# Selective-scan, attention and FFN block: delta split by half-words on VectorE, backward scans that start from the forward y, and a remade plan

## The chip, the core and the metric

The kernel runs on one core of a Trainium2 chip. The metric is the device time of one execution in microseconds (us); a version's time is the median of several runs. A profiled execution is one run more, whose trace is read here.

## What is computed

The input is `x` of 8 images, 96 channels, 64 x 64 points, f32. Layer 0 is a group norm, then a state-space block in four directions, added to `x`; layer 1 is linear attention over the 4096 points of an image and a quantized FFN, each added. What the change touches is in the state-space block:

```python
xs = stack([x_hw, x_wh]); xs = concatenate([xs, flip(xs)])     # 4 directions k: rows, columns, and both reversed
x_dbl = einsum('bkdl,kcd->bkcl', xs, x_proj_w)
dts, Bs, Cs = split(x_dbl, [6, 22], axis=2)
delta = softplus(einsum('bkrl,kdr->bkdl', dts, dt_proj_w) + dt_proj_b)
# scan over l: h = exp(delta * A) * h + delta * u * B;  y = sum_n h * C
out_y = scan(...) + D * u
y = out_y[:, 0] + inv_y[:, 0] + wh_y + invwh_y                 # directions 0 + 2 (reversed) + 1 + 3 (reversed)
y = layernorm(y) * silu(z);  out = y @ out_proj_w.T
```

There are 192 channels d, 16 states n and 4096 points l per direction. The four y's of a point are summed before the layer norm.

## The kernel before

The images are worked in four pairs. For each pair there is a **planned stage** and then a **scan stage**; a last planned stage follows the fourth scan. In a planned stage the part for the next pair (`project`, `convolve`, `prepare`) and the part for the last pair (`back`, `tail`) lie side by side. So there are five planned stages: the first holds only the front part, three middle ones hold both, the last one holds only `back` and `tail`.

*The plan.* In a planned stage every instruction is handed to a `Plan` (lines 57 to 166) with an engine, a cost in us, what it reads and writes, rings of buffers, and a rank. `Plan.run` (line 103) is a list scheduler at build time: it keeps a clock per engine, and of those operations that an engine could begin within 0.1 us of the earliest it takes the one with the lowest rank. The result is a fixed order of instructions per engine; on the chip each engine follows its order and waits where a semaphore is not there yet. The ranks come from six constants (lines 39 to 44): `FRONT`, `CONV` and `PREP` place the projection, the convolution and the preparation on a scale from 0 to 1, `BACK`, `TAIL` and `TAIL_END` the other two parts. A lower rank goes first. All DMAs of the kernel are issued by SP. Most ScalarE instructions of the plan are recorded under line 296 (`act`).

*Preparation* (`prepare`, line 587). 32 sets per pair: 4 directions k, 8 chunks of 512 points. For a set, TensorE forms the states and C, B rows (lines 643, 637), ScalarE copies them, TensorE forms the three delta tiles (lines 662, 657). For each of the three tiles T of [128, 512]: ScalarE softplus gives `d` (f32); VectorE multiplies `d` by u (line 670) and the product is stored in `du`. `d` is then split into three bf16 numbers that add up to it, held in one tile `dp`: ScalarE copies `d` to bf16 (`dp` 0), VectorE subtracts that from `d` (line 681, `rest`), ScalarE copies `rest` to bf16 (`dp` 1), GpSimd subtracts that from `rest` (line 686, `dp` 2). `dp` is stored in `dl`. For directions 1 and 3 GpSimd first writes a transposed copy of the chunk (line 624). The rings hold three `d`, three `dp` and two `rest`; there are 96 tiles per stage.

*Scan* (`scan`, line 696). Written by hand, not planned. 128 steps per pair: direction k, then a block of 128 points; k = 0 and 1 run forward, k = 2 and 3 backward over the blocks. A step has eight scans of 128 x 774 on VectorE (line 853). For each scan, TensorE forms delta * A from the three bf16 parts (six matmuls, line 835), ScalarE takes the exponential (line 842), and for each two scans GpSimd forms delta * u * B (line 817). One step later TensorE sums h * C over the states into PSUM (`sums`, line 858, matmul line 871; eight groups f, two of them in the first of the eight places of a step and none in the last), ScalarE moves the result to `yev` (line 879), and one step after that SP stores it to `ys` (line 889). There are three PSUM buffers `da` for the decay, so the matmuls for scan p + 2 wait for the end of scan p - 1.

*Back* (`back`, line 935). 16 units per pair (8 chunks, 2 images). A unit loads `yk`: four planes of `ys`, one per direction, in pieces of 384 B; directions 0 and 2 are added by VectorE, 1 and 3 by GpSimd (line 982) into `yd`; TensorE transposes and adds both with the identity into PSUM (`turn`, line 996). Then layer norm (line 1015), gate, output projection, residual, norm, keys and values. *Tail* (line 1081): after all units of a pair, attention and FFN; its buffers are laid over those of `yk` and `yd`.

Of the kernel before, what the change touches and what calls it, by code (L numbers as in the profile page):

```python
# [15 lines left out]
ALU = mybir.AluOpType  # L16
# [23 lines left out]
CONV = 0.27  # L40
PREP = 0.15
BACK = 0.63
TAIL = 0.85
TAIL_END = 1.33
# [126 lines left out]
def vss_attn_ffn(ctx: ExitStack, tc: tile.TileContext, a: dict):  # L171
# [233 lines left out]
    def norm(P, n, src_, read, dst, written, new, hold, rank, **kw):  # L405

        mm(P, 0.9, lambda: nc.tensor.matmul(P["ncp" + n][:DIM], c96, src_(), start=True, stop=True),  # L407
           (read, "w_c96"), ("ncp" + n,), (("ncp" + n, hold),), rank)
        act(P, lambda: P["nsq" + n], lambda: P["ncp" + n][:DIM], AF.Square, 0.6, ("ncp" + n,),
            ("nsq" + n,), (("nsq" + n, "small"),), rank)  # L410
        mm(P, 0.9, lambda: nc.tensor.matmul(  # L411
            P["nvp" + n][:DIM], j96, P["nsq" + n], start=True, stop=True),
           ("nsq" + n, "w_j96"), ("nvp" + n,), (("nvp" + n, "q"),), rank)
        root(P, n, "nvp" + n, "nrs" + n, "small", rank)
        dve(P, 0.69, lambda: nc.vector.tensor_tensor(
            dst(), P["ncp" + n][:DIM], P["nrs" + n], ALU.mult, **kw),
            ("ncp" + n, "nrs" + n), written, new, rank)
# [95 lines left out]
    def convolve(P, xi, ybuf, p1, beside):  # L513
# [10 lines left out]
        for h in range(2):  # L524
# [33 lines left out]
            mm(P, 9.0, lambda h=h, ns=ns, taps=taps: taps(h, ns),  # L558
# [28 lines left out]
    def prepare(P, tmp, xi, us, dl, du, bs, cs_, beside):  # L587
# [25 lines left out]
        for o in range(2):  # L613
            for c in range(NCH):
# [14 lines left out]
                for k in (o, o + 2):  # L629
# [13 lines left out]
                    mm(P, 1.9, lambda pt=pt, k=k, u=u, states=states: states(pt, k, u),  # L643
# [18 lines left out]
                    mm(P, 1.2, lambda pqs=pqs, k=k, S=S, steps_=steps_: steps_(pqs, k, S),  # L662
                       (S, *[f"dtw{at}" for at, *_ in places]), pqs, [(q, "q") for q in pqs], rank)
                    P.unit = None
                    for T in range(3):
# [4 lines left out]
                        dve(P, 0.88, lambda q=q, d=d, f=u[T]: nc.vector.tensor_tensor(  # L670
# [5 lines left out]
                        def w(name):  # L676
                            return P[name].rearrange("p (j t) -> p j t", t=WC)

                        act(P, lambda dp=dp: P[dp][:, :, 0], lambda d=d, w=w: w(d), AF.Copy, 0.62, (d,),
                            (dp + "#0",), ((dp, "dp"),), rank)  # L680
                        dve(P, 0.88, lambda rest=rest, d=d, dp=dp, w=w: nc.vector.tensor_tensor(  # L681
                            w(rest), w(d), P[dp][:, :, 0], ALU.subtract), (d, dp + "#0"), (rest,),
                            ((rest, "rest"),), rank)
                        act(P, lambda dp=dp: P[dp][:, :, 1], lambda rest=rest, w=w: w(rest), AF.Copy, 0.63,
                            (rest,), (dp + "#1",), (), rank)
                        P.add("POOL", 1.24, lambda rest=rest, dp=dp, w=w: nc.gpsimd.tensor_tensor(  # L686
                            P[dp][:, :, 2], w(rest), P[dp][:, :, 1], ALU.subtract), (rest, dp + "#1"),
                            (dp + "#2",), (), rank)
# [7 lines left out]
    def scan(dl, du, bs, cs_, ys):  # L696
        with ExitStack() as st:
# [24 lines left out]
            aw, dm, bc, dut, dbu, hs, yev = {}, {}, {}, {}, {}, {}, {}  # L722
# [135 lines left out]
            def sums(s, f):  # L858
# [3 lines left out]
                if f == 0:  # L862
                    yev[s] = trio.tile([128, 2, HQ // 2, NE], F32, name="yev")
                y = yp[f // 4]
                h = hs[s][:, 1:, :].rearrange("p (z i u) r -> p z i u r", z=2, u=SEG)
                w = cw[s // NB % 2][:, :, c % NB].rearrange("p z m (j t) -> p z (m j) t", j=2)
                for i in range(2 * (f % 4), 2 * (f % 4) + 2):
                    for z in range(2):
                        for q in range(4):
                            t = 16 * q + 8 * (f // 4) + i  # L870
                            nc.tensor.matmul(  # L871
                                y[32 * q : 32 * q + 32, 2 * NE * i : 2 * NE * i + 2 * NE]
                                .rearrange("p (j r i) -> p i j r", j=2, r=NR),
                                w[:, z, :, t], h[:, z, :, t : TC : TC // 2, :],
                                start=(i + z == 0), stop=(i + z == 8),
                            )
                if f % 4 == 3:
                    o = 8 * (f // 4)
                    nc.scalar.activation(  # L879
                        yev[s][:, :, o : o + 8, :].rearrange("p j i e -> p i j e"),  # L880
                        y[:, 0 : 16 * NE].rearrange("p (i j e) -> p i j e", j=2, e=NE), AF.Copy,
                    )

            def store(s, j):
                k, c, _ = steps[s]
                v = ys[k, :, c * TC : (c + 1) * TC, :].rearrange(
                    "m (j q i) e -> j q m (i e)", j=2, q=4
                )
                nc.sync.dma_start(v[j], yev[s][j::2, j].rearrange("p i e -> p (i e)"))
# [21 lines left out]
            for s in range(N + 2):  # L911
                for v in range(8):
# [9 lines left out]
                    if s < N:  # L922
                        if v % 2 == 0:
                            fetch(p // 2 + 5)
                        elif v % 4 == 1:
                            load(s + 2, v // 4)
                        if s + 1 < N and steps[s + 1][2] and v % 2 == 1:
# [7 lines left out]
    def back(P, pair, ys, us, zs, t1, tn, tmp, psm, kept=None):  # L935
# [10 lines left out]
        yks = ring(P, tmp, "yk", 2, [128, KD, 8, 4 * NE])  # L946
        yds = ring(P, tmp, "yd", 2, [128, 2, 4, 8 * NE])
# [9 lines left out]
        for i in range(2 * NCH):  # L957
# [4 lines left out]
            yk, yd, z3, ut, xr, yt, g_, ta = (v + n for v in ("yk", "yd", "z3", "ut", "xr", "yt", "g", "ta"))  # L962
            for k in (0, 2, 1, 3):
                v = ys[k, 8 * b : 8 * b + 8]
                if k % 2 == 0:
                    dma(P, 0.4, lambda yk=yk, k=k: P[yk][:, k],
                        lambda v=v, cs=cs: v[:, cs].rearrange("s (p j) e -> p s (j e)", j=4),
                        (), (f"{yk}#{k}",), ((yk, "yk"),), rank)
                else:
                    for h in range(2):  # L970
                        dma(P, 0.2, lambda yk=yk, k=k, h=h: P[yk][64 * h : 64 * h + 64, k],
                            lambda v=v, c=c, h=h: v.rearrange("s (w g j) e -> g w s (j e)", w=HH, j=4)[2 * c + h],
                            (), (f"{yk}#{k}.{h}",), ((yk, "yk"),), rank)
# [7 lines left out]
            for k, name, eng, cost in ((0, "DVE", nc.vector, 0.95), (1, "POOL", nc.gpsimd, 1.8)):  # L981
                P.add(name, cost, lambda eng=eng, k=k, yd=yd, yk=yk: eng.tensor_tensor(  # L982
                    P[yd][:, k].rearrange("p j (s e) -> p s j e", s=8),
                    P[yk][:, k].rearrange("p s (j e) -> p s j e", j=4),
                    P[yk][:, k + 2].rearrange("p s (j e) -> p s j e", j=4), ALU.add),
                    [f"{yk}#{j}" for j in ((0, 2) if k == 0 else ("1.0", "1.1", "3.0", "3.1"))],
                    (f"{yd}#{k}", "yk"), ((yd, "yd"),), rank)

            def turn(yd, k, g, py):
                for j in range(4):  # L990
# [3 lines left out]
                    else:  # L994
                        o = o.rearrange("p (g j w) -> p g j w", g=2, j=4)[:, :, j]
                    nc.tensor.matmul(  # L996
                        o, P[yd][:, k, j, DIM * g : DIM * g + DIM], ident,
                        start=(k + j == 0), stop=(k + j == 4),
                    )

            for k in range(2):
                for g in range(2):
                    py = f"py{g}" + n
                    mm(P, 1.0, lambda yd=yd, k=k, g=g, py=py, turn=turn: turn(yd, k, g, py), (f"{yd}#{k}",),
                       (py,), ((py, "q"),), rank)
# [11 lines left out]
            mm(P, 1.8, lambda mean=mean, yt=yt, both=both: both(mean, yt, lambda g: j192),  # L1017
# [6 lines left out]
            mm(P, 1.8, lambda yv=yv, g_=g_, both=both: both(yv, g_, lambda g: j192),  # L1024
# [9 lines left out]
            mm(P, 1.8, lambda po=po, g_=g_, both=both: both(po, g_, lambda g: woT[:, g]),  # L1034
# [8 lines left out]
            for h in range(2):  # L1043
# [16 lines left out]
                mm(P, 0.7, lambda pk=pk, to=to, h=h, keys=keys: keys(pk, to, h), (to,), (pk,), ((pk, "q"),), rank)  # L1060
# [18 lines left out]
        return yks, yds  # L1079

    def tail(P, pair, t1, tn, spare, kept):
        flat = [t.rearrange("p k s e -> p (k s e)") for t in spare[0]]
        P.ring("t2", [v[:DIM, F * j : F * j + F] for j in range(2) for v in flat])
        P.ring("ot", [v[:DIM, 2 * F : 3 * F] for v in flat])
        P.ring("xa", [v[:DIM, 3 * F : 4 * F] for v in flat])
        half_ = [t.rearrange("p k j e -> p (k j e)") for t in spare[1]]
        P.ring("hq", [v[:, 0 : 3 * F // 4].bitcast(F8).rearrange("p (m f) -> p m f", f=F) for v in half_])
        P.ring("h16", [v[:, F * j : F * j + F // 2].bitcast(F16) for j in (1, 2) for v in half_])
        P.ring("y16", [v[:DIM, 768 : 768 + F // 2].bitcast(F16) for v in half_])
        P.ring("tq", [v[:DIM, 384 : 384 + F // 4].bitcast(F8) for v in half_])  # L1090
        P.ring("turn", [None] * 3)
        for i in range(2 * NCH):
# [12 lines left out]
            mm(P, 0.9, lambda pa=pa, b=b, tf=tf: nc.tensor.matmul(  # L1105
# [5 lines left out]
            for m in range(3):  # L1111
                p1, h16 = f"pf{m}" + n, f"h16{m}" + n
                mm(P, 0.45, lambda p1=p1, m=m, tq=tq: nc.tensor.matmul(  # L1113
# [12 lines left out]
            mm(P, 1.35, lambda p2=p2, hq=hq, second=second: second(p2, hq),  # L1126
# [17 lines left out]
    for pair in range(npair + 1):  # L1144

        new = {}
        if pair < npair:
            for name, shape, dtype in (
# [3 lines left out]
                ("cs", [KD, NT // NB, 2 * NS, NB * TC], F32), ("ys", [KD, 16, L, NE], F32),  # L1152
                ("t1", [2, DIM, L], F32), ("tn", [2, DIM, L], F32),
            ):
                new[name] = dram.tile(shape, dtype, name=name)
        with ExitStack() as st:
# [20 lines left out]
            if old:  # L1177
                if not new:
                    kept = [[tmp.tile([DIM + i, L], F32, name=f"kept{i}{b}") for b in range(2)] for i in range(2)]
                spare = back(P, pair - 1, old["ys"], old["us"], old["zs"], old["t1"], old["tn"], tmp, psum, kept)  # L1180
                tail(P, pair - 1, old["t1"], old["tn"], spare, kept)
# [132 lines left out]
```

## Time and profile before

| what | us |
|---|---|
| median of 3 runs (lowest, highest) | 10320.08 (10318.13, 10324.31) |
| the profiled execution | 10309.3 |
| its span, first to last instruction | 10307.5 |
| the four scan stages together | 7109.6 |
| planned stages: first, three middle, last | 549.4, 774.2, 758.9, 769.8, 345.6 |
| busy in the span: PE, DVE, ACT, POOL | 7289.4, 9045.2, 7000.9, 8011.6 |

How to read the profile: PE is TensorE's matmuls, PEld its weight loads, DVE VectorE, ACT ScalarE, POOL GpSimd, SP the engine that issues the DMAs. A line of a group reads: source line, engine, operation, output tile <- input tiles, shape, count, busy time in us, mean duration in ns, idle time of the engine just ahead of these instructions, and what ended most of it. An f32 matmul shows as two records. In tile names `A` is the large buffer that holds the tiles of preparation, `q` a PSUM buffer. A scan stage is taken here from its first to its last instruction of line 853. "Granted clock" is the share of TensorE's full clock in a stretch; "DMA share" is the mean busy share of the core's 16 DMA engines.

### The profile page before, as it was taken

The page shows a single profiled execution, that of the slowest core. Times are in us where ns is not written, and L with a number is a line of the kernel's source. Part 1 is how long each engine was busy: PE and PEld are TensorE (multiplying, and loading weights), DVE is VectorE, ACT ScalarE, POOL GpSimd, SP SyncE. Part 2 cuts the span into 40 slices and gives each one's busy share as a digit, 9 for nine tenths or more (in the row PEclk, how much of TensorE's full clock was granted, in tenths as well). Part 3 has the DMA queues.
Part 4 walks back from the last instruction along what each step waited for, and adds up shares of the span by engine and source line. Part 5 has one row for each costly group of instructions (what it writes and reads, how often), then busy time and mean ns, then how long its engine had stood idle before and what let it go on. Part 6 is the DMA issues. An engine that isn't in the chain of part 4 may idle for free. (4 is left out here: it accounts for less than half of the span.)

```text
span 10307.5 us, 383249 instructions
## 1 busy us (share of the span) xinstructions
PE 7289.4 (71%) x166080; PEld 5185.1 (50%) x166080; DVE 9045.2 (88%) x6688; ACT 7000.9 (68%) x12268; POOL 8011.6 (78%) x2800
## 2 busy tenths in 40 slices
PE   6766666768866666676886666767688567666678
PEld 2155555654315555555432555656543255555554
DVE  6589999997579999999767999999866799999985
ACT  5667777776566777776666777777666677777754
POOL 2499999991259999999125999999713699999971
PEclk7579999898868999989986989898898798999999
DMA  4878887876778888887787788888767788888885
GB/s 127 226 210 214 213 216 212 218 203 146 209 205 210 215 213 217 213 217 189 171 210 203 213 217 212 217 212 217 194 165 206 200 214 214 214 215 216 214 193 104
DMA packets 1593918, 2085.12 MB, mean 202 GB/s; under 512 B 409891, under 2 KB 1050404, under 8 KB 1588644
## 3 DMA queue, kind: packets, MB, share of 16 engines
q1 hardware_dynamic: 1592228, 2060.59, 76.6%
q8 instruction: 1304, 21.36, 1.0%
q14 instruction: 386, 3.16, 0.1%
HBM read 1601.99 MB, written 458.04 MB: 200 GB/s over the span
## 5 line engine op out<-in xcount | busy, mean ns | idle before, releaser
L853 DVE TENSOR_TENSOR_SCAN h<-da,dbu 128x774 f32<-128x774 f32 x4096 | 7026.6, 1759 | 168.1 <-POOL dbu L817 33.1
L817 POOL TENSOR_TENSOR dbu<-dut,bc 128x1536 f32<-128x1536 f32 x2048 | 7081.8, 3572 | 71.8 <-DMA dm<-dl 35.9
L842 ACT ACTIVATE da<-da 128x768 f32<-128x768 f32 x4092 | 3260.7, 797 | 1983.9 <-PE da L835 1969.5
L835 PE MATMUL da<-dm,aw 128*128 128x128 bf16 x24576 | 2281.5, 235 | 2347.3 <-DVE h L853 2081.8
L835 PEld LDWEIGHTS <-aw 128*128 128x128 bf16 x24576 | 1792.2, 104 | 2595.2 <-issue 2308.8
L871 PE MATMUL yp<-h,cw 128*32 128x48 f32 x131072 | 2899.2, 238 | 83.7 <-issue 70.3
L871 PEld LDWEIGHTS yp<-h,cw 128*32 128x32 f32 x131072 | 2409.0, 154 | 528.6 <-issue 207.5
L771 ACT ACTIVATE cw<-bc,blk 128x512 f32<-128x512 f32 x2048 | 1473.1, 721 | 73.0 <-DMA bc<-cs 54.7
L686 POOL TENSOR_TENSOR A<-A 128x512 bf16<-128x512 f32 x384 | 489.2, 1280 | 954.5 <-ACT A L296 912.0
L296 ACT ACTIVATE A<-A 128x512 bf16<-128x512 f32 (+1 forms) x777 | 466.4, 620 | 274.0 <-DVE A L681 228.4
L982 POOL TENSOR_TENSOR yd<-yk 128x768 f32<-128x768 f32 x64 | 120.8, 1888 | 655.3 <-PE q L996 306.4
L879 ACT ACTIVATE yev<-yp 128x384 f32<-128x384 f32 x1024 | 504.7, 493 | 74.6 <-PE yp L871 74.3
L681 DVE TENSOR_TENSOR A<-A 128x512 f32<-128x512 f32 x384 | 324.2, 851 | 174.7 <-ACT A L296 135.7
L814 ACT COPY dbu<-h 128x12 f32<-128x12 f32 x1984 | 409.3, 206 | 0.0
L657 PE MATMUL q<-A 6*64 6x512 f32 x1536 | 331.6, 779 | 74.3 <-ACT A L296 70.4
L624 POOL COPY A<-A 128x512 f32<-128x512 f32 x96 | 142.5, 1504 | 307.8 <-ACT A L296 277.3
L540 DVE SCALAR_TENSOR_TENSOR A<-A,c_convw,A 128x2048 f32<-128x2048 f32 x128 | 299.1, 2355 | 0.6
L996 PEld LDWEIGHTS q<-ident,yd 128*96 128x96 f32 x2048 | 238.6, 165 | 84.1 <-issue 53.1
L670 DVE TENSOR_TENSOR A<-A 128x512 f32<-128x512 f32 x192 | 203.8, 1080 | 77.3 <-ACT A L296 70.8
L996 PE MATMUL q<-ident,yd 128*96 128x128 f32 x2048 | 255.1, 276 | 17.3 <-DVE yd L982 9.5
L637 PE MATMUL q<-A 128*64 128x512 f32 x512 | 209.5, 935 | 77.3 <-ACT A L296 56.6
L296 ACT ACTIVATE small<-hold 96x512 f32<-96x512 f32 x192 | 112.7, 590 | 218.5 <-PE hold L407 218.3
(125 smaller groups left out, 5446.5 us busy)
## 6 DMA issues: line engine op xcount, KB each, us to landing
dut<-du SPq DMA_DIRECT2D x2048, 384.0 KB
dm<-dl SPq DMA_DIRECT2D x1024, 288.0 KB
dl<-A SPq DMA_DIRECT2D x256, 384.0 KB
dm<-dl SPq DMA_DIRECT2D x1024, 96.0 KB
ys<-yev SPq DMA_DIRECT2D x1024, 96.0 KB
du<-A SPq DMA_DIRECT2D x256, 256.0 KB
bc<-cs SPq DMA_DIRECT2D x512, 128.0 KB
bc<-bs SPq DMA_DIRECT2D x512, 128.0 KB
```

What stands on the lines that cost most here:

```text
L296: "ACT", cost, lambda: nc.scalar.activation(dst(), src_(), func, **kw),
L657: nc.tensor.matmul(P[pqs[T]][o : o + 64], dtw[at : at + RK, k, o : o + 64], P[S][at : at + RK], start=True, stop=True,)
L686: P.add("POOL", 1.24, lambda rest=rest, dp=dp, w=w: nc.gpsimd.tensor_tensor(P[dp][:, :, 2], w(rest), P[dp][:, :, 1], ALU.subtract), (rest, ...
L771: nc.scalar.activation(cw[i % 2][:, :, :, m, :].rearrange("p z j t -> p (z j) t"), bc[i][:, 1].rearrange("p z (j t) -> p (z j) t", j=NB), ...
L814: nc.scalar.copy(start, segs(hs[s - 1][:, :, r])[:, :, :, 1 if back else TC])
L817: nc.gpsimd.tensor_tensor(segs(t)[:, :, :, 1:], dut[g].unsqueeze(1) .to_broadcast([128, 2, NI, TC]), bc[s // NB][:, 0, :, bass.ts(c % NB, ...
L835: nc.tensor.matmul(e[:, i], aw[k, r][:, i, z, :], dm[s // 2][:, NI * r + i, bass.ts(c % 2, TC)], start=True, stop=True,)
L842: nc.scalar.activation(e, e, AF.Exp)
L853: nc.vector.tensor_tensor_scan(hs[s][:, w, r][:, d], da[p % 3][:, o : o + W6][:, d], dbu[4 * s + r][:, w][:, d], 0.0, ALU.mult, ALU.add,)
L871: nc.tensor.matmul(y[32 * q : 32 * q + 32, 2 * NE * i : 2 * NE * i + 2 * NE] .rearrange("p (j r i) -> p i j r", j=2, r=NR), w[:, z, :, t], ...
L879: nc.scalar.activation(yev[s][:, :, o : o + 8, :].rearrange("p j i e -> p i j e"), y[:, 0 : 16 * NE].rearrange("p (i j e) -> p i j e", j=2 ...
L996: nc.tensor.matmul(o, P[yd][:, k, j, DIM * g : DIM * g + DIM], ident, start=(k + j == 0), stop=(k + j == 4),)
```

## The change

1. *Delta split.* The first part of `d` is no longer a rounded copy but its upper 16 bits, read in place as bf16 with a step of two. VectorE subtracts the upper half of `d` from `d` (`rest`), and then the upper half of `rest` from `rest` straight into `dp` 2. ScalarE copies the two upper halves to `dp` 0 and `dp` 1. GpSimd has no part in it.
2. *Backward scans.* `ys` becomes four tensors, one per direction, with groups of four points innermost. In a step with k >= 2 SP loads the y of direction k - 2 for the same block (`recall`, in the last of the eight places, for the next step), and TensorE adds it into the sums through the identity, once per half of the groups, as the first matmul of the accumulation. So `ys` of directions 2 and 3 hold the sum with 0 and 1. `yev` has two buffers for three, and its ScalarE copy is now contiguous.
3. *Back and tail.* A unit loads two planes of `ys` for four; the adds of line 982 and `yd` go; `turn` takes its weights from `yk` with a step of four elements. Tail has buffers of its own.
4. *Plan.* Costs of matmuls and of three VectorE operations are given other values, and all ranks but `FRONT`.

```diff
-CONV = 0.27
-PREP = 0.15
-BACK = 0.63
-TAIL = 0.85
-TAIL_END = 1.33
+CONV = 0.57
+PREP = 0.27
+BACK = 0.55
+TAIL = 0.92
+TAIL_END = 1.56
...
-            mm(P, 9.0, lambda h=h, ns=ns, taps=taps: taps(h, ns),
+            mm(P, 10.5, lambda h=h, ns=ns, taps=taps: taps(h, ns),
...
-                    mm(P, 1.9, lambda pt=pt, k=k, u=u, states=states: states(pt, k, u),
+                    mm(P, 2.85, lambda pt=pt, k=k, u=u, states=states: states(pt, k, u),
...
-                    mm(P, 1.2, lambda pqs=pqs, k=k, S=S, steps_=steps_: steps_(pqs, k, S),
+                    mm(P, 2.1, lambda pqs=pqs, k=k, S=S, steps_=steps_: steps_(pqs, k, S),
...
-                        act(P, lambda dp=dp: P[dp][:, :, 0], lambda d=d, w=w: w(d), AF.Copy, 0.62, (d,),
+                        def high(name):
+                            return P[name].bitcast(BF16).rearrange("p (j t o) -> p j t o", t=WC, o=2)[:, :, :, 1]
+
+                        dve(P, 0.66, lambda rest=rest, d=d, w=w, high=high: nc.vector.tensor_tensor(
+                            w(rest), w(d), high(d), ALU.subtract), (d,), (rest,), ((rest, "rest"),), rank)
+                        act(P, lambda dp=dp: P[dp][:, :, 0], lambda d=d, high=high: high(d), AF.Copy, 0.56, (d,),
                             (dp + "#0",), ((dp, "dp"),), rank)
-                        dve(P, 0.88, lambda rest=rest, d=d, dp=dp, w=w: nc.vector.tensor_tensor(
-                            w(rest), w(d), P[dp][:, :, 0], ALU.subtract), (d, dp + "#0"), (rest,),
-                            ((rest, "rest"),), rank)
-                        act(P, lambda dp=dp: P[dp][:, :, 1], lambda rest=rest, w=w: w(rest), AF.Copy, 0.63,
+                        dve(P, 0.66, lambda rest=rest, dp=dp, w=w, high=high: nc.vector.tensor_tensor(
+                            P[dp][:, :, 2], w(rest), high(rest), ALU.subtract), (rest,),
+                            (dp + "#2",), ((dp, "dp"),), rank)
+                        act(P, lambda dp=dp: P[dp][:, :, 1], lambda rest=rest, high=high: high(rest), AF.Copy, 0.56,
                             (rest,), (dp + "#1",), (), rank)
-                        P.add("POOL", 1.24, lambda rest=rest, dp=dp, w=w: nc.gpsimd.tensor_tensor(
-                            P[dp][:, :, 2], w(rest), P[dp][:, :, 1], ALU.subtract), (rest, dp + "#1"),
-                            (dp + "#2",), (), rank)
...
-                    yev[s] = trio.tile([128, 2, HQ // 2, NE], F32, name="yev")
+                    yev[s] = wk.tile([128, 2, 2, 8 * NE], F32, name="yev")
...
+                second = steps[s][0] >= 2
+                if second and f % 4 == 0:
+                    nc.tensor.matmul(
+                        y[:, 0 : 16 * NE].rearrange("p (j n) -> p j n", j=2), ident,
+                        yin[s][:, f // 4].unsqueeze(1).to_broadcast([128, 2, 8 * NE]), start=True, stop=False,
+                    )
...
-                                start=(i + z == 0), stop=(i + z == 8),
+                                start=(i + z == 0 and not second), stop=(i + z == 8),
...
+            def recall(s):
+
+                if s >= N or steps[s][0] < 2:
+                    return
+                k, c, _ = steps[s]
+                yin[s] = wk.tile([128, 2, 8 * NE], F32, name="yin")
+                v = ys[k - 2][:, c * HQ : (c + 1) * HQ].rearrange("m (j q a) e b -> j q m (a e b)", j=2, q=4)
+                for j in range(2):
+                    nc.sync.dma_start(yin[s][j::2].rearrange("p h n -> p (h n)"), v[j])
...
+                        elif v == 7:
+                            recall(s + 1)
...
-        yks = ring(P, tmp, "yk", 2, [128, KD, 8, 4 * NE])
-        yds = ring(P, tmp, "yd", 2, [128, 2, 4, 8 * NE])
+        ring(P, tmp, "yk", 2, [128, 2, 8, 4 * NE])
...
-            for k in (0, 2, 1, 3):
-                v = ys[k, 8 * b : 8 * b + 8]
+            for k in range(2):
+                v = ys[k + 2][8 * b : 8 * b + 8]
...
-                    nc.tensor.matmul(
-                        o, P[yd][:, k, j, DIM * g : DIM * g + DIM], ident,
-                        start=(k + j == 0), stop=(k + j == 4),
-                    )
+                    w = P[yk][:, k].rearrange("p s (e j) -> p j (s e)", j=4)[:, j, DIM * g : DIM * g + DIM]
+                    nc.tensor.matmul(o, w, ident, start=(k + j == 0), stop=(k + j == 4))
...
+            new["ys"] = [dram.tile([16, L // 4, NE, 4], F32, name=f"ys{k}") for k in range(KD)]
```

## The prediction

> **What bounds the kernel now.** I first read the order of work from the scan line's first and last instruction in each pair, then the busy time of each stage by windows, then who waits for whom inside a stage.
>
> ```profile
> L853 DVE TENSOR_TENSOR_SCAN h<-da,dbu 128x774 f32<-128x774 f32 x4096 | 7026.6, 1759 | 168.1 <-POOL dbu L817 33.1
> L817 POOL TENSOR_TENSOR dbu<-dut,bc 128x1536 f32<-128x1536 f32 x2048 | 7081.8, 3572 | 71.8 <-DMA dm<-dl 35.9
> L842 ACT ACTIVATE da<-da 128x768 f32<-128x768 f32 x4092 | 3260.7, 797 | 1983.9 <-PE da L835 1969.5
> L681 DVE TENSOR_TENSOR A<-A 128x512 f32<-128x512 f32 x384 | 324.2, 851 | 174.7 <-ACT A L296 135.7
> L686 POOL TENSOR_TENSOR A<-A 128x512 bf16<-128x512 f32 x384 | 489.2, 1280 | 954.5 <-ACT A L296 912.0
> ```
>
> The scans run from 549.4 to 2328.4, 3102.6 to 4879.8, 5638.7 to 7413.9 and 8183.7 to 9961.9 us: 7109.6 us of the 10307.5. There VectorE and GpSimd have next to no idle time; a step of eight scans takes 13.83 us in nearly every step. Neither line is touched by the change. All that can be won lies in the other 3197.9 us, the five planned stages. The windows of these, and of a backward half of a scan stage (columns: length, busy time of PE, PEld, DVE, ACT, POOL, granted clock, DMA share, GB/s):
>
> ```profile
> 0.00:549.40 549.40, 353.48 (x1402) 96.21 (x1403) 340.59 (x351) 311.41 (x509) 211.81 (x153) 0.67 0.66 178
> 2328.40:3102.60 774.20, 597.98 (x2874) 251.99 (x2875) 494.50 (x638) 491.59 (x799) 224.96 (x171) 0.80 0.73 188
> 9961.90:10307.50 345.60, 300.71 (x1472) 163.15 (x1472) 191.23 (x328) 143.49 (x258) 55.32 (x34) 0.92 0.65 129
> ```
> ```profile
> 1440.00:2328.00 888.00, 613.51 (x19458) 526.26 (x19457) 879.59 (x514) 632.76 (x1138) 884.07 (x263) 0.90 0.80 210
> ```
> ```profile
> 2588.00:3078.00 490.00, 382.89 (x1372) 139.42 (x1370) 315.82 (x444) 321.79 (x542) 189.96 (x137) 0.77 0.77 204
> 2340.00:2440.00 100.00, 81.15 (x300) 42.63 (x301) 52.58 (x84) 59.96 (x92) 12.91 (x14) 0.89 1.04 228
> 9970.00:10180.00 210.00, 197.30 (x974) 123.70 (x975) 118.47 (x167) 72.32 (x130) 34.51 (x18) 0.97 1.01 195
> ```
>
> In a middle stage no engine is full: even PE is busy 598 of 774 us. Such a stage is bound by chains in a fixed order. Its last 490 us hold the preparation (32 sets of delta); its first 100 us have full DMA queues. The last stage's first 210 us are full on PE and DMA together. Who waits in the 490 us:
>
> ```profile
> POOL A L686 <- ACT A L296: 260.6, 61, 29.4
> ACT A L296 <- DVE A L681: 52.6, 44, 8.7
> PEld q L657 <- ACT A L296: 45.2, 35, 5.2
> ```
>
> ScalarE stands 52.6 us for the first remainder on VectorE, because its next conversion is queued behind that round trip; PE then stands for ScalarE.
>
> **The delta split.** Now each of 96 tiles per stage goes softplus, ACT copy, VectorE remainder, ACT copy, GpSimd remainder: five steps in a chain. After, the first remainder needs softplus alone, the second needs the first, and both ACT copies lie beside them. GpSimd loses 96 x 1.28 = 123 us per stage; it was idle for most of the stage, so by itself this is worth nothing. VectorE gains 96 subtractions. L681 (same shape, one bf16 operand) has median 0.685 us, and where GpSimd runs at the same time I find 1.158 us. So 66 us are added. Against that L670 (89.5 us in the first middle stage) and L681 (79.6) lose most of their overlap with L686: at 0.685 each they would take 66 + 66, 37 less; and two-tensor adds L982 leave VectorE, 16 x 0.96 = 15 us. Net +14 us, on an engine busy 495 of 774: I count it as nothing, hidden under PE's 598; uncovered it costs 14. The ACT copies read 16-bit halves instead of f32; nearest rows 0.595 (f32 from PSUM) and 0.625 us: -0.03 to 0 on 192 copies, at most -6 us, taken as 0.
>
> The gain is the stall: of the 52.6 us ScalarE waits, the first copy no longer waits for VectorE at all and the second waits only if VectorE is behind. I take three quarters, 40 us; bounds 0 (something else in the chain is as late) and 53. In the first stage the same wait is 70.1 us in total, but there DMA is next: packets occupy 0.87 of the 16 engines between 230 and 510 us, so no more than 0.13 x 280 = 36 us can go. I take 22, bounds 0 and 36.
>
> The Trainium skill, "GPSIMD Engine Reference", section 1 (Specifications), says that GpSimd shares its SBUF interfaces with VectorE and collides with VectorE instructions that have two SBUF inputs. The 0.685 against 1.158 us agree. By that rule the new subtraction would still cost 1.158 us wherever GpSimd's transposing copies L624 (34 us per stage) run, some 14 us more per stage than I count.
>
> **Half the reads of ys.** The back part now reads two planes of y instead of four. Per stage 32 x 384 KB + 64 x 192 KB = 65,536 packets of 384 B, about 33 ns each, over 16 engines: 135 us of queue time, of which 67 go. In 2340 to 2440, where the queues are full, these packets hold 0.60, so up to 30 us of it can come free; PE is busy 81 of these 100 us, so I take 15, bounds 0 and 30. In the last stage's first 210 us these packets hold 0.69 of a full queue, but PE works back to back (197 of 210), so the queue's relief ends at PE: I count only the shorter first load, 0.8 MB at 195 GB/s = 4, taken as 5 us, bounds 0 and 13 (PE's idle time there). GpSimd's and VectorE's adds (16 x 1.9 and 16 x 0.96 us) lay beside PE: nothing. The weights of L996 are now read with a step of four elements. L871 already loads weights with a step of 64 elements and issues a 48-column matmul every 22 ns, so I take 0; worst case each of 512 loads takes 0.165 us in the open instead of the 0.11 between starts, 28 us per stage.
>
> **The backward scans.** 256 of 512 steps gain two DMAs of 96 KB and two identity matmuls of 384 f32 columns. A 512-column f32 matmul is two records that start 0.43 us apart at full clock (L1015 near 10,090 us): 384 columns cost 2 x 0.32 = 0.64 us, 1.3 per step; 64 steps put 82 us on PE's 613 of 888: it fits. The DMAs add 128 packets of 1,536 B at 73 ns / 16 = 0.58 us per 13.83: share 0.80 to 0.84. On SP's queue recall stands behind the fetch of the same step, which already waits for GpSimd (110 us of queue waits in that half), and its own wait is for matmuls half a step older: nothing behind it is held. A y store's last packet lands 3.9 us after issue (95% under 6.9); recall is issued nine scans, 15.5 us, before its use.
>
> What matters is lateness: behind the identity on PE wait the decay matmuls L835, then the exponential L842, then the scan. The exponential of a step's fourth scan, which follows the double group of sums, ends 1.70 us (median; 95% over 1.26) before its scan starts. 0.64 us fits. But PE falls to half clock for 3.4 us in about every second step (45 intervals in that half), and there the identity costs 1.28. The margins lie between 0.15 (the smallest, at the sixth scan) and 2.0; spread evenly, 1.28 exceeds them by 0.35 on average (1.13 x 1.13 / 2 / 1.85). 128 such steps, and an interval covers one of the two identities in about half of them (2 x 3.4 / 13.83): 128 x 0.35 x 0.49 = 22. I take +20; bounds 0 and +110 (256 x 0.43, 1.28 beyond a margin of 0.85, the lowest twentieth at the sixth scan).
>
> The skill, "TensorE: Matmul & The Clock Gate", Part 1, says that the clock halves after an idle window of about 3.4 us and returns after a busy one. The 3.4 us intervals agree. By that rule the added work would fill those windows and the 20 us would be 0; no run here shows it.
>
> **Remade plan.** Costs of the planner and ranks set only the order. Two were far off: the matmul groups issued at lines 643 and 662 were planned at 1.9 and 1.2 us; L637 takes 92.3 / 32 = 2.9 and L657 72.7 / 32 = 2.3; they are now 2.85 and 2.1. No row prices an order: bounds +65 (one more hole as between the second and third set of the first middle stage, 65 us) and -65 by symmetry. I take -5 per middle stage, 0 elsewhere.
>
> **Sum** against the profiled execution, 10309.3 us (span 10307.5): middle stages 3 x (40 + 15 + 5) = 180, first 22, last 5, scans +20: -187, so 10122. The median shown is 10.8 above that execution: **10133 us**.
>
> **Rivals.**
> - *Hidden anyway* (0.19): PE at half clock sets the pace of preparation (clock 0.77, busy 78%) and the freed waits come back as PE waits. Only 15 + 0 per middle stage, 5 + 5 elsewhere, scans +20: -35, 10285, with its own range 10220 to 10299. For it: PE is the busiest engine; against: PE itself waits for ScalarE.
> - *More* (0.11): the full 53 + 30 + some 20 of order per middle stage, 36 first, 13 last, scans 0: -358, 9962. For it: gaps on PE feed its own half clock.
> - *Slower* (0.12): the identity matmul makes the backward scans wait. Place: PE's queue ahead of L835. Price: both on the path are 1.42 us (clock 0.9) x 256 = +364; with the 207 won elsewhere 10477. It decides from 207 / 256 = 0.81 us per step, that is when lateness eats the 1.70 us margin and 0.81 more. Against: DVE idle for ACT is 0.3 us in the half shown, so the margin holds today.
> - *Same* (0.06): gains of the hidden case and a scan stall near 0.3 us per step.
>
> **How the numbers follow.** The forecast's own case, 9990 to 10220, has 0.52. Within 0.2% of 10320 is 10299 to 10341, about what a measurement can tell from no change. Faster 0.52 + 0.19 + 0.11 = 0.82, same 0.06, slower 0.12. The range 9970 to 10320 leaves out half of "more", half of "same" and the slower case, near 0.2.
>
> **What would show it.** Right: scan stages still 1775 to 1800 us with L853 at 1759 ns; no L686; L681 and the new line near 0.69 us; ACT waiting for DVE in preparation under 15 us; middle stages near 705 to 720, the first near 525, the last near 340. Wrong: backward halves over 910 us with DVE waiting for ACT; L996 above 276 ns; middle stages unchanged because PE or the order holds them; or the last stage falling by far more than 13 us, which would mean that DMA and not PE held it.

## The result and the profile after

The changed kernel takes 10467.99 us (median of 4 runs, 10465.71 to 10481.06) against 10322.19 for the kernel before on the same chip: ratio 1.0142, 95% interval 1.0125 to 1.016. It is slower, where 10133 was forecast. Its profiled execution took 10481.06 us, with a span of 10479.3. Split as before, from the first to the last instruction of the scans:

| us | before | after | difference | forecast |
|---|---|---|---|---|
| first planned stage | 549.4 | 530.5 | -18.9 | -22 |
| three middle stages, sum | 2302.9 | 2092.3 | -210.6 | -180 |
| last stage | 345.6 | 371.2 | +25.6 | -5 |
| four forward halves | 3561.6 | 3565.8 | +4.2 | 0 |
| four backward halves | 3547.9 | 3919.3 | +371.4 | +20 |

Together the planned stages gave what was forecast (-203.9 for -207); the backward halves took it back almost twice. From the page after, the groups that answer to those of before (the scan, the product that feeds it, the exponential, the two remainders):

```profile
L855 DVE TENSOR_TENSOR_SCAN h<-da,dbu 128x774 f32<-128x774 f32 x4096 | 7027.9, 1759 | 501.7 <-POOL dbu L819 378.5
L819 POOL TENSOR_TENSOR dbu<-dut,bc 128x1536 f32<-128x1536 f32 x2048 | 7092.1, 3527 | 427.7 <-DMA dut<-du 231.7
L844 ACT ACTIVATE da<-da 128x768 f32<-128x768 f32 x4092 | 3259.0, 797 | 2167.0 <-PE da L837 2155.8
...
L682 DVE TENSOR_TENSOR A<-A 128x512 f32<-128x512 f32 x384 | 278.6, 731 | 91.6 <-ACT A L296 90.1
L686 DVE TENSOR_TENSOR A<-A 128x512 bf16<-128x512 f32 x384 | 279.6, 729 | 71.9 <-DMA dl<-A 71.1
```

No instruction of the scans became longer: the scan is still 1759 ns, and GpSimd's product even shortened. What is new stands in the last columns: VectorE idles 378.5 us for GpSimd (33.1 before), and GpSimd idles 231.7 us for the DMA that loads `dut` (7.9 before). The windows of the first, the second and the last planned stage, and of the first backward half (columns as in the prediction):

```profile
0.00:530.50 530.50, 344.76 (x1402) 97.35 (x1403) 365.47 (x447) 309.43 (x509) 96.44 (x57) 0.68 0.68 184
2400.80:3094.30 693.50, 575.64 (x2876) 274.63 (x2877) 489.32 (x718) 495.76 (x806) 82.83 (x59) 0.87 0.73 192
10108.10:10479.30 371.20, 329.78 (x1474) 198.11 (x1474) 174.84 (x312) 147.39 (x258) 25.42 (x18) 0.92 0.35 86
1424.00:2400.00 976.00, 731.52 (x19706) 563.70 (x19702) 877.66 (x512) 629.85 (x1135) 884.39 (x261) 0.84 0.75 204
```

The last line is the telling one. The half is 88 us longer, VectorE and GpSimd have the busy time that they had, PE's 731 of 976 leaves room, and the DMA engines are *less* full than before (0.75 for 0.80, 204 GB/s for 210) although more is to be moved. Nothing in these columns is the bound; what is left is the one engine that they don't show, SP, which issues the DMAs. Its own waits, first in a backward half before (1440 to 2328 us; L790 is the fetch of `dut`):

```profile
SPq L790 <- POOL dbu L817: 115.6, 88, 2.8
SPq L889 <- ACT yev L879: 16.0, 2, 11.3
SPq L777 <- DMA dm<-dl: 8.3, 12, 1.1
```

and after (1440 to 2400 us; L779 loads `cw`, L745 `dm`, L895 stores `ys`, L792 is the fetch):

```profile
SPq L779 <- DMA dut<-du: 42.7, 66, 1.6
SPq L745 <- DMA dm<-dl: 22.6, 51, 0.9
SPq L895 <- DMA yin<-ys: 21.0, 29, 1.1
SPq L792 <- DMA bc<-bs: 18.8, 29, 1.4
SPq L895 <- DMA bc<-bs: 18.3, 29, 0.9
...
SPq L792 <- POOL dbu L819: 9.1, 26, 0.6
```

Before, SP came early to the fetch and stood 115.6 us until GpSimd gave a buffer free: that was its slack. After, this wait is 9.1 us; SP comes late. It now waits for landings of *other* tiles: a load of `cw` waits for a `dut`, a store of `ys` for a `yin`. These are no data dependences: each issue takes one of eight semaphores in turn, and in the trace's records none starts before the DMA eight issues earlier has landed (all 904 issues of steps 6 to 56 of this half wait for the semaphore that they then use).

For the experiments I use, besides the length of a backward half, two shares of SP's time, read from the records of the issues: *issuing* (an issue takes some 0.4 to 0.7 us) and *held* (the issue ahead is done, and it starts within 0.2 us of the landing eight issues earlier). Steps 6 to 56 of the first backward half (the landing is the mean from the start of the issue); the length is the mean of the four halves. The kernels x4, x13, z1, z2 and w1 were run four to nine times, the other experiments once; the lengths are those of one profiled execution each:

| kernel | half, us | DMAs per step | issue to landing, us | issuing | held | sum |
|---|---|---|---|---|---|---|
| before | 887.0 | 16 | 5.6 | 0.73 | 0.05 | 0.78 |
| after | 979.8 | 18 | 6.3 | 0.71 | 0.24 | 0.95 |
| x1 loads, no identity | 981.2 | 18 | 6.3 | 0.71 | 0.24 | 0.95 |
| x2 identity, no loads | 894.3 | 16 | 5.8 | 0.71 | 0.09 | 0.80 |
| x3 quarter-size recalls | 932.4 | 18 | 5.5 | 0.77 | 0.17 | 0.94 |
| x4 `dm` in fewer, larger loads | 988.8 | 16 | 7.3 | 0.61 | 0.35 | 0.96 |
| x5 recalls from ScalarE | 1074.7 | 18 | 5.4 | 0.58 | 0.38 | 0.96 |
| x6 half the `cw` loads | 932.8 | 16 | 7.0 | 0.65 | 0.31 | 0.96 |
| x7 18 issues in each step | 975.6 | 18 | 6.2 | 0.72 | 0.22 | 0.95 |
| x10 recall in one DMA | 934.6 | 17 | 6.4 | 0.69 | 0.26 | 0.95 |
| x13 x10, and half of `cw` on ScalarE | 897.1 | 15 | 6.7 | 0.65 | 0.17 | 0.82 |

(In x5 SP issues 16 of the 18, and the earlier landing is that of the DMA before it on the same semaphore.) The last column sorts the kernels: 0.78 to 0.82 where the half is 887 to 897 us, 0.94 to 0.96 wherever it is longer. SP's queue is full there.

### The profile page after: what moved, and what is told of

Same layout as the page of the kernel before. It is cut to its first block, busy times and chain, and to the rows that moved or that the text cites. A ratio compares the mean times of both kernels' runs of the same rounds, so it can differ in the third digit from the quotient of the medians.

```text
span 10479.3 us, 385469 instructions
## 1 busy us (share of the span) xinstructions
PE 7755.9 (74%) x167104; PEld 5451.5 (52%) x167104; DVE 9038.6 (86%) x7008; ACT 7013.4 (67%) x12289; POOL 7456.9 (71%) x2352
## 5 line engine op out<-in xcount | busy, mean ns | idle before, releaser
L855 DVE TENSOR_TENSOR_SCAN h<-da,dbu 128x774 f32<-128x774 f32 x4096 | 7027.9, 1759 | 501.7 <-POOL dbu L819 378.5
L819 POOL TENSOR_TENSOR dbu<-dut,bc 128x1536 f32<-128x1536 f32 x2048 | 7092.1, 3527 | 427.7 <-DMA dut<-du 231.7
L871 PE MATMUL yp<-yin,ident 128*128 128x384 f32 x1024 | 560.0, 635 | 0.6 <-issue 0.6
L1138 POOL TENSOR_TENSOR ot<-t,y 96x512 f32<-96x512 f32 x64 | 116.7, 1824 | 608.8 <-DVE y L1136 561.4
L296 ACT ACTIVATE A<-A 128x512 bf16<-128x512 bf16 (+1 forms) x777 | 445.2, 618 | 134.5 <-DMA dl<-A 105.6
L1007 PEld LDWEIGHTS q<-ident,yk 128*96 128x96 f32 x2048 | 379.7, 271 | 69.4 <-issue 43.4
L1007 PE MATMUL q<-ident,yk 128*96 128x128 f32 x2048 | 381.9, 339 | 11.7 <-DMA yk<-ys 9.3
L682 DVE TENSOR_TENSOR A<-A 128x512 f32<-128x512 f32 x384 | 278.6, 731 | 91.6 <-ACT A L296 90.1
L686 DVE TENSOR_TENSOR A<-A 128x512 bf16<-128x512 f32 x384 | 279.6, 729 | 71.9 <-DMA dl<-A 71.1
L657 PE MATMUL q<-A 6*64 6x512 f32 x1536 | 280.9, 760 | 48.1 <-ACT A L296 46.0
L296 ACT ACTIVATE A<-q,c_dtb 128x512 f32<-128x512 f32 x384 | 252.7, 679 | 4.0 <-PE q L657 3.2
L411 PE MATMUL q<-small,c_j 96*96 96x512 f32 x384 | 227.3, 685 | 33.2 <-ACT small L296 24.0
```

The costliest lines, as they stand in the source:

```text
L296: "ACT", cost, lambda: nc.scalar.activation(dst(), src_(), func, **kw),
L819: nc.gpsimd.tensor_tensor(segs(t)[:, :, :, 1:], dut[g].unsqueeze(1) .to_broadcast([128, 2, NI, TC]), bc[s // NB][:, 0, :, bass.ts(c % NB, ...
L855: nc.vector.tensor_tensor_scan(hs[s][:, w, r][:, d], da[p % 3][:, o : o + W6][:, d], dbu[4 * s + r][:, w][:, d], 0.0, ALU.mult, ALU.add,)
L871: nc.tensor.matmul(y[:, 0 : 16 * NE].rearrange("p (j n) -> p j n", j=2), ident, yin[s][:, f // 4].unsqueeze(1).to_broadcast([128, 2, 8 * N ...
L1007: nc.tensor.matmul(o, w, ident, start=(k + j == 0), stop=(k + j == 4))
```

## The experiments

**Which half of the recall costs?** Two runs, each with one half.

```diff
-                second = steps[s][0] >= 2
+                second = False
```

> The changed kernel with its two recall DMAs per backward step kept and the identity matmul left out (so the forward y is missing from the output). Theory 1 (the two extra DMA issues per step: the sync engine issues in order and each issue waits until the DMA eight issues earlier has landed, so the load of du is issued late, GpSimd is late, VectorE's scan is late): the backward halves stay at 960 to 985 us, the span near 10470. Theory 2 (the extra bytes, 512 KB per step, slow the transfers): the same 960 to 985. Theory 3 (the recorded rival: the identity matmul makes TensorE late for the scan): the halves fall to 885 to 895, the span to about 10110.

10485.1 us, halves 979.1, 985.5, 984.1, 976.2. Without any identity matmul the whole loss is there, so TensorE is not its cause. (The extra bytes are 192 KB per step, two DMAs of 96 KB; the 512 KB named above are too many.)

```diff
+                if s > 2 * NT + 1:
+                    yin[s] = yin[s - 2]
+                    return
                 yin[s] = wk.tile([128, 2, 8 * NE], F32, name="yin")
```

> The changed kernel with the identity matmuls kept and the recall DMAs issued only in the first two steps of a backward half, whose tiles all later steps read (so the y that is added is that of the wrong steps). Theory 1 and theory 2: backward halves 885 to 900 us, span about 10120. Theory 3: 960 to 985, span near 10470. If both the DMAs and the matmul are needed for the loss, both this run and the one without the identity fall to about 890.

10128.17 us, halves 895.1, 893.2, 892.5, 896.2: with the matmuls and without the DMAs 7 us of 93 remain. The waits of VectorE for GpSimd in the first backward half, x1 first, then x2:

```profile
DVE h L855 <- POOL dbu L819: 83.6, 64, 2.2
```
```profile
DVE h L855 <- POOL dbu L819: 2.8, 10, 0.7
```

Theory 3, the recorded rival, has fallen. Theories 1 and 2 both fit.

**Number or bytes?**

```diff
+                if s > 2 * NT + 1:
+                    yin[s] = yin[s - 2]
...
+                    if s > 2 * NT + 1:
+                        nc.sync.dma_start(yin[s][j:32:2].rearrange("p h n -> p (h n)"), v[j, 0])
```

> The changed kernel with both recall DMAs per backward step, each moving a quarter of its rows (so three quarters of the forward y added are stale). The number of DMAs is that of the changed kernel, the extra bytes a quarter. Theory 1 (number of issues): the backward halves stay above 930 us. Theory 2 (bytes): they fall to 885 to 905. Theory 3: 960 to 985.

10283.65 us, halves 928.1 to 938.0: half of the loss went, on the edge of theory 1 and outside theory 2. With fewer bytes all DMAs land sooner (5.5 for 6.3 us), but two small loads, with the matmuls, still cost 45 us per half, 7 of them the matmuls' (x2).

```diff
-                w = NE // 4
-                o = 2 * w * (s % 2) + w * part
+                if part:
+                    return
+                w = NE // 2
+                o = w * (s % 2)
```

> The changed kernel with the loads of dm for the planned stages issued once per step in a double width instead of twice, so that a step of the scans issues two DMAs fewer and moves the same bytes; it computes the same. Theory 1: the backward halves fall to 885 to 905 us, the span to about 10110 to 10180, which is faster than the kernel before (0.98 to 0.987 of it). Theory 2 and theory 3: the backward halves stay at 960 to 985, the time near 10470 (1.014).

10569.89 us, ratio 1.0236 (1.0219 to 1.0253): a miss for theory 1 as I had put it. Two issues fewer, and the backward halves are 9 us *longer*; even the forward ones rose, from 891 to 906. The loads of `dm`, now 576 and 192 KB for 288 and 96, land 8.3 us after the end of their issue (median; 5.8 in the changed kernel), and what stands behind them lands later too (`dut` 7.4 for 5.7), and the held share rises to 0.35. So the number alone is not the currency. What fills the queue is issue time plus waiting for a turn, and the second was longer where the DMAs ahead were larger.

```diff
                     m += 8
+                    if s > 2 * NT + 3 and m % 2:
+                        yield
+                        continue
                     nc.sync.dma_start(
```

> The changed kernel with every second of the small loads of cw (16 KB each, eight per two steps) left out in the backward halves after their first steps, so that half of those diagonal weights are stale there. Per two steps 32 DMAs instead of 36, and 64 KB less of some 6260 KB. Theory 1 (number of issues: the sync engine's queue is full, its own issue time and the waits for the DMA eight issues earlier): the backward halves fall from 977 to 885 to 915 us. Theory 2 (bytes: a step of 3.13 MB in 13.83 us would need 226 GB/s, and the transfers give 205 to 214): they fall by 1 % at most, 965 to 980.

10283.38 us, halves 929.9 to 935.5. Loads of 16 KB with some 1% of the bytes gave back half of the loss. Theory 2 has fallen; theory 1 expected yet more. The DMA then moved 214 GB/s (1480 to 2320 us) where the changed kernel moved 205.

**Can the queue be relieved without leaving work out?**

```diff
-                    nc.sync.dma_start(yin[s][j::2].rearrange("p h n -> p (h n)"), v[j])
+                    nc.scalar.dma_start(yin[s][j::2].rearrange("p h n -> p (h n)"), v[j])
```

> The changed kernel with the two recall DMAs of a backward step issued from ScalarE's queue instead of the sync engine's; it computes the same. Theory 1 in the form that the sync engine's own issue time is what counts (two issues of 0.56 us per step leave its queue): the backward halves fall to 900 to 945 us. Theory 1 in the form that the eight DMAs in flight count: they stay at 955 to 985, since the recalls take their turns among the same eight, and ScalarE may be held by its own issues. Theory 2 (bytes): 965 to 985.

10848.53 us, halves 1071.2 to 1077.6: worse than either form expected. The recalls take their turns among the same eight, but ScalarE issues them late (96 of 100 in the eighth scan of VectorE's step, where SP had issued 99 of 100 in the second to fourth), and SP is held until they have landed:

```profile
SPq L745 <- DMA yin<-ys: 83.9, 45, 5.6
SPq L779 <- DMA yin<-ys: 64.6, 21, 5.2
SPq L746 <- DMA yin<-ys: 50.5, 25, 5.7
```

The Trainium skill, "DMA: Bandwidth & Descriptors", section "Issuing engines are not separate DMA queues", says that issuing from several engines saves only the time that the sequencer needs, usually small beside the DMA. One recall in the changed kernel takes 0.56 us to issue and lands 6.3 us later, which agrees, as does that the move brought no gain; but the issues together fill 0.71 of SP's time. The further loss of 95 us per half comes from the turns: 0.24 of SP's time goes behind recalls in x5, 0.04 in the changed kernel.

```diff
...
-                    if v == 0:
-                        more = diagonal(s + 1) if s % NB else load_bc(s + NB)
+                    if v == 0 and s % NB:
+                        rest = diagonal(s + 1)
+                        more = itertools.islice(rest, 6)
+                    elif v == 0:
+                        more = itertools.chain(load_bc(s + NB), rest)
```

> The changed kernel with the loads of bc and cw spread evenly over the two steps of a pair: 18 DMA issues in each step instead of 20 and 16; it computes the same, with the same DMAs in all. If the loss comes from the peak of 20 issues in every second step: the backward halves fall to 890 to 930 us. If the queue is full on the mean (theory 1 as I read the trace: of 920 us the sync engine issues in 661 and waits for the DMA eight earlier in 220) or the bytes set it (theory 2): 960 to 985.

10601.47 us, backward halves 974.0 to 977.6: the queue is full on the mean, not in a peak. The whole is slower since the last loads of `cw` now come too late for the sums in the forward halves as well (925 to 934 us; PE waits 54.6 us for `cw` in the first).

```diff
...
-                for j in range(2):
-                    nc.sync.dma_start(yin[s][j::2].rearrange("p h n -> p (h n)"), v[j])
+                nc.sync.dma_start(yin[s].rearrange("p h n -> p (h n)"), ys[k - 2][c])
...
```

> The changed kernel with the forward y kept in a layout of its own, one row per partition, so that a backward step recalls it by one DMA of 192 KB instead of two of 96 KB; it computes the same. Per backward step 17 DMAs instead of 18, the same bytes. If the number of issues counts as the runs with fewer small loads showed (16 per step: 933 us instead of 978): the backward halves take 945 to 962 us. If only the bytes count: 970 to 985. If a larger DMA holds its turn for longer, as the merged loads of dm did: 985 to 1000.

10297.96 us, halves 932.5 to 937.3: the same bytes in one DMA fewer gave back 45 us, more than expected. The issue of 192 KB takes 0.38 us (median) for two of 0.56, and it lands 6.3 us after that, as the small ones did; one turn is saved whole.

```diff
                     m += 8
+                    if k >= 2 and m % 2:
+                        nc.scalar.activation(
+                            cw[i % 2][:, :, :, m, :].rearrange("p z j t -> p (z j) t"),
+                            bc[i][:, 1].rearrange("p z (j t) -> p (z j) t", j=NB),
+                            AF.Copy, scale=blk[:, m : m + 1],
+                        )
+                        yield
+                        continue
                     nc.sync.dma_start(
...
```

> The changed kernel with the recall as one DMA and, in the backward halves, four of the eight small cw loads per two steps written by ScalarE instead (0.717 us each there, 1.4 us more per step on an engine that is busy for 11 of 13.83); it computes the same. Per backward step 15 DMAs instead of 18, the bytes nearly the same. If issues and bytes both count (the one step fewer and the two fewer each give back some of the 90 us): backward halves 900 to 920 us and the whole 10170 to 10240, faster than the kernel before (0.985 to 0.993). If only bytes count: 965 to 980. If ScalarE becomes late for VectorE: over 930 with VectorE waiting for ScalarE.

10167.72 us against 10326.89: ratio 0.9848 (0.9832 to 0.9864), faster than both kernels and a little beyond the best case expected, with halves of 894.9 to 900.9. All of the forward y is recalled and added. The first backward half, and SP's and VectorE's waits in it:

```profile
1427.00:2321.00 894.00, 676.38 (x19706) 533.19 (x19705) 878.04 (x512) 698.40 (x1260) 884.27 (x263) 0.95 0.86 220
```
```profile
SPq L800 <- POOL dbu L827: 111.5, 101, 2.2
```
```profile
DVE h L863 <- POOL dbu L827: 4.2, 19, 0.3
```

SP again comes early and waits 111.5 us for GpSimd, as before the change; ScalarE carries the four blocks (698 for 630 us); and the DMA moves 220 GB/s. With it the byte theory is gone for good: nearly the same bytes as in the changed kernel, in 894 us instead of 976. No run had more than eight turns, so what a ninth would be worth is open.

**What gave the planned stages their gain?** Three kernels between before and after: the kernel before with the split alone (z1),

```diff
-                        dve(P, 0.88, lambda rest=rest, d=d, dp=dp, w=w: nc.vector.tensor_tensor(
-                            w(rest), w(d), P[dp][:, :, 0], ALU.subtract), (d, dp + "#0"), (rest,),
...
-                        P.add("POOL", 1.24, lambda rest=rest, dp=dp, w=w: nc.gpsimd.tensor_tensor(
...
+                        dve(P, 0.66, lambda rest=rest, dp=dp, w=w, high=high: nc.vector.tensor_tensor(
+                            P[dp][:, :, 2], w(rest), high(rest), ALU.subtract), (rest,),
```

> The kernel before with the new delta split alone (costs of the other operations in the plan and the outputs as before). If the split carries the gain of the planning (recorded as 40 us per middle stage and 22 in the first): middle stages 715 to 735 us instead of 768, first stage 527 to 532, the whole 10150 to 10190. If the gain is the reads': middle stages 755 to 770, the whole 10280 to 10310.

with the ranks and the planner costs of the matmuls alone (z2; the cost of L670 stays as before, here and in w1),

```diff
-CONV = 0.27
-PREP = 0.15
+CONV = 0.57
+PREP = 0.27
...
-                    mm(P, 1.9, lambda pt=pt, k=k, u=u, states=states: states(pt, k, u),
+                    mm(P, 2.85, lambda pt=pt, k=k, u=u, states=states: states(pt, k, u),
```

> The kernel before with the new costs of the plan alone, delta split and outputs as before. Recorded: 5 us less per middle stage, anything within 65 thinkable. If the plan matters little: middle stages 750 to 775 us, the whole 10270 to 10330. If the new order of the stages carries the gain: middle stages 700 to 730, the whole 10130 to 10210.

and with both edits at once (w1):

> The kernel before with the new delta split and the new costs of the plan, but with the two forward and two backward outputs kept and read apart as before: no recall, no identity, no strided weights. Backward halves 886, first stage about 530, last stage about 345 (the last stage of the changed kernel, 371, is put down to the strided weights). What the middle stages show tells the changed kernel's 697 us apart: if the split and the plan carry nearly all of the gain, they take 700 to 725 us and the whole 10110 to 10170, faster than both kernels; if the halved reads of the outputs carry half of it or more, 730 to 760 us and 10200 to 10280.

| kernel | first | middle, mean | last | us (before 10304.74) | ratio (interval) |
|---|---|---|---|---|---|
| before | 549.4 | 767.6 | 345.6 | | |
| z2 plan | 538.6 | 781.8 | 343.0 | 10337.01 | 1.0027 (1.0017 to 1.0037) |
| z1 split | 527.8 | 737.9 | 352.1 | 10197.13 | 0.9891 (0.9877 to 0.9906) |
| w1 split and plan | 530.0 | 750.8 | 344.0 | 10225.24 | 0.9919 (0.9905 to 0.9934) |
| after | 530.5 | 697.4 | 371.2 | | |

The split alone gives 30 us per middle stage, a little less than the 715 to 735 expected of it. The new costs *lose* 13 to 14 there, with the old split and with the new: z2 lies above both of its ranges. w1 lies in its second, where the outputs carry half or more of the gain: from w1 to after the middle stage falls by 53 more. That is the outputs' part under the new plan; whether the new plan loses time with the new outputs too was not run. w1's backward halves take 887.8 us, as before, and its last stage is 27 us shorter than that of after.

## Why the prediction was wrong, step by step

- **"Nothing behind it is held": the step that failed.** I looked for a wait of the recall itself, found none, and priced its bytes as a DMA share of 0.80 going to 0.84 (it fell to 0.75). The queue that it joins was never summed up. Before, of a step of 13.84 us SP issued for 10.1 and was held for 0.8; the 115.6 us in 888 that it waited for GpSimd, 1.8 us per step, were its slack. I had read these queue waits as a reason why nothing more would be held. After, SP issues for 10.9 us per step and is held for 3.7: together 14.7, more than the 13.84 that a step took, and the step takes 15.4. Measured: +371 us in four halves, or 1.4 us per step. The two issues of 0.56 us alone would have fitted into the 1.8; the held time did not, and no row of the kernel before gives its price.
- **The identity matmul, +20 (0 to 110):** right. x2, which has it without the loads, takes 7.3 us per half more than before, 29 in all. In the four halves VectorE waits 23.7 us for ScalarE, 2.7 before: 21 of the 29 come by the path that was forecast. The first half (1440 to 2320 us), before, then x2:

```profile
DVE h L853 <- ACT da L842: 0.3, 1, 0.3
```
```profile
DVE h L855 <- ACT da L844: 6.5, 5, 2.8
```

  The Trainium skill ("TensorE: Matmul & The Clock Gate", Part 1) has the clock halve after an idle window and return after a busy one, from which the prediction also worked out a cost of 0, with the idle windows filled. They were not: the granted clock from 1460 to 2300 us is 0.91 in x2 and 0.90 before.
- **The slower rival** gave 10477, close to the time measured, but by lateness on TensorE. x1 has no identity and the same time. Its number was luck, and the 0.12 was given to a mechanism that isn't there.
- **The delta split, -40 per middle stage (0 to 53), -22 in the first:** right in mechanism, too large by a quarter: z1 gives -30 and -21.6. In the first middle stage ScalarE's wait for VectorE fell from 52.6 us to 3.6 in z1, but its wait for TensorE's states (L637) rose from 43.9 to 53.3. In the first stage the wait for VectorE went from 70.1 us to none and that for the DMA that stores `dl` rose from 20.8 to 60.6: the bound that was forecast there. The subtractions of the changed kernel have medians of 0.684 and 0.682 us, as read from L681 (0.685); the mean is 0.73, so the clash of VectorE with GpSimd (the 1.158 us, and the Trainium skill, "GPSIMD Engine Reference", section 1) costs little here.
- **Halved reads, -15 per middle stage (0 to 30):** mis-sized. With the adds that go with them, the outputs' part is worth -53 (w1 to after, under the new plan), more than the upper bound of 30. I had priced the adds of L982 as hidden beside PE; how the 53 divide between reads, adds and buffers was not tried.
- **Strided weights, 0 (worst 28 per stage):** the last stage took 25.6 us more, near the worst case, but not for its reason, a load of 0.165 us in the open: the load itself grew. The loads went from 165 to 271 ns and the matmuls from 276 to 339:

```profile
L1007 PEld LDWEIGHTS q<-ident,yk 128*96 128x96 f32 x2048 | 379.7, 271 | 69.4 <-issue 43.4
...
L1007 PE MATMUL q<-ident,yk 128*96 128x128 f32 x2048 | 381.9, 339 | 11.7 <-DMA yk<-ys 9.3
```

  In the last stage PE's busy time on this line rose from 68.0 to 95.8 us at the same granted clock of 0.92. PE holds that stage (330 of 371 us), and its DMA share fell from 0.65 to 0.35 without any gain. No run has the strided weights alone. My row for it, L871 before with its step of 64 elements, showed starts between matmuls and not the load's own time.
- **The plan, -5 (65 either way):** the sign was wrong, +13 to +14 with the outputs as before, inside its bounds.

In sum the scans were forecast at +20 and came to +376, which is more than the planned stages' -204.

## What to carry to other kernels

Before a DMA is added to a steady loop, add up how the queue that issues it spends a step: issuing, held for a turn, waiting for a free buffer. Only the last is slack, here 1.8 of 13.84 us. The new DMAs take their issue time out of it (1.1 us here), and the held time can grow on top (0.8 to 3.7 us here). The share of the DMA engines does not tell: it was 0.75 with the queue full and 0.86 with room in it (x13). If the queue is full, save whole DMAs: of the 93 us, one of 96 KB per step gave back 45 (x10) and two of 16 KB gave back 47 (x6). Merging loads that are already large, or issuing from another engine, made it worse here.

## What was not expected of the hardware

- A DMA of 16 KB takes a turn for 4.0 us, one of 96 KB (`yin`) for 6.3 and one of 192 KB for 6.3 (medians, end of issue to landing, steps 6 to 56, in after and x10), so the small ones cost far more than their bytes.
- The DMA rate in a backward half was 204 GB/s in the changed kernel and 220 in x13, with nearly the same bytes: the lower figure was the issuing queue's, not the transfers'. Why a landing takes 5 to 7 us at all is not settled here.
- A weight load of 96 f32 columns takes 165 ns when they lie together and 271 ns with a step of four elements.
